# The start-up of a fused recurrent mixer and gated FFN: four token tiles normalised together, the first FFN step split into high and low parts, inverse roots by Newton steps, loads reordered

## The chip, the core and the metric

The kernel runs on one core of one Trainium2 chip. The metric is the device time of one execution in microseconds (us), the median of several runs. A core has five engines that run side by side, each with its own instruction queue worked off in order: the tensor engine (PE), VectorE (DVE), ScalarE (ACT), GpSimd (POOL) and SyncE (SP), which issues most of the DMA transfers. PE writes into PSUM, eight banks that the kernel hands out as small pools of tiles; the other engines work from PSUM and from the on-chip SBUF.

## The reference

A layer on x of 4 sequences x 256 tokens x 512 features. It is normalised, goes through a state-space mixer (128 heads, chunks, eight groups) and through a gated FFN whose weights are integers from -1 to 1 with a scale for each row; the product of both is added to x.

```python
def _layernorm(x, axis=-1, eps=1e-05):
    m = jnp.mean(x, axis=axis, keepdims=True)
    v = jnp.var(x, axis=axis, keepdims=True)
    return (x - m) / jnp.sqrt(v + eps)
...
gate_out = x_flat @ gate_w.T          # 1024 x 1792
up_out = x_flat @ up_w.T
hidden = jax.nn.silu(gate_out) * up_out
out_flat = hidden @ down_w.T
...
x = L0_attn_hidden_states
xn = _layernorm(x, axis=-1)
s = _L0_attn_ref(xn, ...)
g = _silu(_L0_ffn_ref(xn, ...))
x = x + s * g
```

The change touches the normalisation and the beginning of the FFN; the mixer is only moved in time with them.

## The kernel before

The 1024 tokens are 8 token tiles of 128 (`xts[0]` to `xts[7]`). The function `front` holds everything up to the FFN's end, about the first 300 us; the mixer's main loop over 64 tiles of channels follows it. Both are scheduled by hand: each engine works in the order in which the program issues to it.

**The entrance** (L519 to L550). SP loads x of tiles 0 to 3, the three weight blocks of FFN step 0 (`load_ffn(0)`: gate wg, up wu, down wd, each 256 KB of int32), two scale vectors, x of tiles 4 to 7, step 1's weights, the small constants, and `w` for the first mixer products. While x is on its way, PE runs matmuls on a tile of ones (`busy`, L270). The loop at L537 then normalises one tile after the other: statistics on DVE (`ln_stats`, L249 and L250), the root on ACT (`ln_std`, L253), the reciprocal on DVE (L542), the normalisation on DVE (`ln_norm`, L256), the transposition on PE (`ln_turn`, L264) into a PSUM tile. One turn later `split_tile` copies this into the high part xh on ACT (L283, rounded to the type that PE takes at full rate) and subtracts for the low part xl on DVE (L284). `keep` (L268) copies the transposed tile in full precision into `xnT` on ACT. The weight casts (`cast_ffn`, L230) run on POOL.

**The FFN steps** (L562 to L589). `steps` are 28: two halves of 512 tokens (tiles 0 to 3, then 4 to 7) by 14 blocks of 128 FFN features. A step multiplies wg with xh and xl into one PSUM bank (`project_exact`, L290: for each of four k a product with xh, then one with xl), takes Silu of it on ACT (L567), multiplies wu the same way, joins both on DVE (sg, L576), and splits sg into hh (ACT, L584) and hl (DVE, L588). The down product of a step (L298) comes two steps later, through `pending`. Each step issues the loads of step n + 2 at its head and the casts of step n + 1 in its middle. The pool `f2` of loaded weights holds two buffers for each of the three blocks.

**Other work between.** At three places of each step `next(pieces)` issues the next turn of a generator. Turns 0 and 1 (`first_pieces`, L385) are the statistics of tiles 4, 5 and 6, 7; turn 2 their common root on ACT, its reciprocal on DVE and the norm of tile 4; turn 3 the norm of tile 5; turns 4 and 5 the norms of tiles 6 and 7, and the transposition and keep of tiles 4 and 5; turns 6 and 7 the transposition and keep of tiles 6 and 7. These four transpositions share one PSUM bank (`ps_t`), so each waits until the keep before it has emptied it. From turn 6 on come the product with `wdt` and the steps of dt (`dt_pieces`), from turn 11 on the mixer's shared B and C blocks (`bc_pieces`).

Where turn 2 stands in a step, and what is queued around it:

```python
pu, wd = project_exact(ws[1], xh, xl), ws[2]
...
nc.vector.scalar_tensor_tensor(sg, pu, us[:, f:f + 1], sg, ALU.mult, ALU.mult)
if n + 1 < len(steps):
    ws = cast_ffn(n + 1)
next(pieces, None)
...
nc.scalar.copy(hh, sg)
...
next(pieces, None)
nc.vector.tensor_tensor(hl, sg, hh.bitcast(F32), ALU.subtract)
```

Of the kernel before, what the change touches and what calls it, by code (L numbers as in the profile page):

```python
# [43 lines left out]
F32 = mybir.dt.float32  # L44
F32R = mybir.dt.float32r
I32 = mybir.dt.int32
AF = mybir.ActivationFunctionType
ALU = mybir.AluOpType
PSUM = bass.MemoryType.PSUM

P = 128
# [4 lines left out]
NT = T // P  # L56
HID = 512
KT = HID // P
# [3 lines left out]
G = 8  # L62
# [3 lines left out]
CT = DIN // P  # L66
# [7 lines left out]
EPS = 1e-5  # L74
LEAD = 10
EARLY = 10
HALF = T // 2
# [5 lines left out]
def mixer_ffn(ctx: ExitStack, tc: tile.TileContext, x, in_w, conv_w, conv_b, dt_bias, a_log, d_col,  # L83
              norm_w, out_w, gate_t, up_t, down_t, gate_s, up_s, down_s, out):
    nc = tc.nc

    const = ctx.enter_context(tc.tile_pool(name="const", bufs=1))
    small = ctx.enter_context(tc.tile_pool(name="small", bufs=3))
    dram = ctx.enter_context(tc.tile_pool(name="dram", bufs=1, space=bass.MemoryType.DRAM))
    ps_proj = ctx.enter_context(tc.tile_pool(name="ps_proj", bufs=3, space=PSUM))  # L90
# [5 lines left out]
    eps = const.tile([P, 1], F32, name="eps")  # L96
# [5 lines left out]
    tiny = const.tile([P, 1], F32, name="tiny")  # L102
# [29 lines left out]
    def load_w(*tiles):  # L132
        w = wp.tile([P, 2, KT, P], F32, name="w")
        for n, i in enumerate(tiles):
            nc.sync.dma_start(w[:, n], in_w[i])
        return w
# [57 lines left out]
    def front(pre, one_of, fp, f2, hp, ep):  # L194
# [14 lines left out]
        bias = one_of.tile([P, 1], F32, name="bias")  # L209
# [4 lines left out]
        steps = [(h, f) for h in range(2) for f in range(FT)]  # L214
        loads = {}

        def load_ffn(n):
            f, ts = steps[n][1], []
            for tag, src in (("wg", gate_t[f]), ("wu", up_t[f]),
                             ("wd", down_t[f * P:(f + 1) * P, :])):  # L220
                wi = f2.tile([P, HID], I32, name=f"{tag}_i", tag=f"{tag}_i")
                nc.sync.dma_start(wi, src)
                ts.append((tag, wi))
            loads[n] = ts

        def cast_ffn(n):
            ws = []
            for tag, wi in loads.pop(n):
                w = fp.tile([P, HID], F32R, name=tag, tag=tag, bufs=4 if tag == "wd" else 2)
                nc.gpsimd.tensor_copy(w, wi)  # L230
                ws.append(w)
            return ws


        xts = []

        def load_x(ts):
            for t in ts:
                xt = pre.tile([P, HID], F32, name="xt")
                nc.sync.dma_start(xt, x[t * P:(t + 1) * P, :])  # L240
                xts.append(xt)

        mv = one_of.tile([P, NT, 2], F32, name="mv")
        rstd = one_of.tile([P, NT], F32, name="rstd")
        nc.scalar.activation(rstd[:, 0:1], eps, AF.Sqrt)

        def ln_stats(t):
            st = small.tile([P, 6], F32, name="st")
            nc.vector.bn_stats(st, xts[t])  # L249
            nc.vector.bn_aggr(mv[:, t, :], st)  # L250

        def ln_std(t, n=1):
            nc.scalar.activation(rstd[:, t:t + n], mv[:, t:t + n, 1], AF.Sqrt, bias=eps)  # L253

        def ln_norm(t):
            nc.vector.tensor_scalar(xts[t], xts[t], mv[:, t, 0:1], rstd[:, t:t + 1],  # L256
                                    ALU.subtract, ALU.mult)

        def ln_turn(t):

            p, tag = ((ps_o, "o"), (ps_y, "y"))[t // 2] if t < 4 else (ps_t, "t")
            tp = p.tile([P, KT, P], F32, name="tp", tag=tag)
            for k in range(KT):
                nc.tensor.transpose(tp[:, k, :], xts[t][:, k * P:(k + 1) * P], ident)  # L264
            return tp

        def keep(t, tp):
            nc.scalar.copy(xnT[:, :, t * P:(t + 1) * P], tp)  # L268

        def busy(n):  # L270

            for _ in range(n):
                nc.tensor.matmul(idle, ones, ones, start=True, stop=True)
# [4 lines left out]
        def split_x():  # L278
            return [hp.tile([P, KT, HALF], F32R, name=n) for n in ("xh", "xl")]

        def split_tile(xh, xl, t, v):
            to = slice(t % 4 * P, (t % 4 + 1) * P)
            nc.scalar.copy(xh[:, :, to], v)  # L283
            nc.vector.tensor_tensor(xl[:, :, to], v, xh[:, :, to].bitcast(F32), ALU.subtract)  # L284

        def project_exact(w, xh, xl):
            pp = ps_proj.tile([P, HALF], F32, name="pp", tag="proj")
            for k in range(KT):
                for part in (xh, xl):
                    nc.tensor.matmul(pp, w[:, k * P:(k + 1) * P], part[:, k, :],  # L290
                                     start=(k == 0 and part is xh),
                                     stop=(k == KT - 1 and part is xl))
            return pp
# [24 lines left out]
        held = {}  # L318
# [61 lines left out]
        def combine_x(n):  # L380

            a, b = ((x12, x11), (x22, xc[:, 0]), (x22, x12), (x21, xc[:, 1]))[n]
            nc.vector.tensor_sub(xc[:, n], a, b)

        def first_pieces():  # L385
            for t in range(4, NT):
                ln_stats(t)
                if t % 2:
                    yield
            ln_std(4, 4)  # L390
            nc.vector.reciprocal(rstd[:, 4:], rstd[:, 4:])
            ln_norm(4)
            yield
            ln_norm(5)
            yield
            for t in range(4, NT):
                if t + 2 < NT:
                    ln_norm(t + 2)
                keep(t, ln_turn(t))
                yield  # L400
            yield
            for n in range(4):
                combine_x(n)
                if n == 0:
                    held["a"] = combine_w(held.pop("w"))
                yield
# [113 lines left out]
        load_ffn(0)  # L520
        nc.sync.dma_start(gs, gate_s)
        nc.sync.dma_start(us, up_s)
        load_x(range(4, NT))
        load_ffn(1)
        nc.sync.dma_start(wdt, in_w[PROJ // P - 1])
        nc.sync.dma_start(bias, dt_bias)
        nc.sync.dma_start(a_neg, a_log)
        for to, src in ((cw, conv_w), (cb, conv_b), (dcol, d_col), (nw, norm_w)):
            nc.sync.dma_start(to, src)
        nc.sync.dma_start(ds_bc, down_s.partition_broadcast(P))  # L530
        held["w"] = load_w(2 * CT + G, 2 * CT)

        idle = ps_t.tile([P, P], F32, name="idle", tag="t")
        xh, xl = split_x()
        busy(8)
        ws, tps = cast_ffn(0), []
        for t in range(5):  # L537
            if t < 4:
                ln_stats(t)
                ln_std(t)  # L540
            if t:
                nc.vector.reciprocal(rstd[:, t - 1:t], rstd[:, t - 1:t])  # L542
                ln_norm(t - 1)
                tps.append(ln_turn(t - 1))
                busy(4)
            if t > 1:
                split_tile(xh, xl, t - 2, tps[t - 2])
        split_tile(xh, xl, 3, tps[3])
        for t in range(4):
            keep(t, tps[t])  # L550
        pending = []

        def down_next():
# [6 lines left out]

        pfs = None
        for n, (h, f) in enumerate(steps):  # L562
            if n + 2 < len(steps):
                load_ffn(n + 2)
            pg = project_exact(ws[0], xh, xl)
            sg = fp.tile([P, HALF], F32, name="sg")
            nc.scalar.activation(sg, pg, AF.Silu, scale=gs[:, f:f + 1])  # L567
            if f == 2 and h:
                ffn_out(h - 1, pfs, (2, 3))
            next(pieces, None)  # L570
            pu, wd = project_exact(ws[1], xh, xl), ws[2]
            if f == FT - 1 and h == 0:
                xh, xl = split_x()
                for t in range(4, NT):
                    split_tile(xh, xl, t, xnT[:, :, t * P:(t + 1) * P])
# [4 lines that stand above are left out]
            if len(pending) == 2:  # L580
                down_next()
            hh = fp.tile([P, HALF], F32R, name="hh")
            hl = fp.tile([P, HALF], F32R, name="hl")
            nc.scalar.copy(hh, sg)  # L584
            if f == 1 and h:
                ffn_out(h - 1, pfs, (0, 1))
            next(pieces, None)
            nc.vector.tensor_tensor(hl, sg, hh.bitcast(F32), ALU.subtract)  # L588
            pending.append((f, hh, hl, wd))  # L589
        w = load_w(1, CT + 1)  # L590
# [6 lines left out]

    with (tc.manual_schedule(), tc.tile_pool(name="pre", bufs=NT) as pre,
          tc.tile_pool(name="one_of", bufs=1) as one_of, tc.tile_pool(name="fp", bufs=3) as fp,
          tc.tile_pool(name="f2", bufs=2) as f2, tc.tile_pool(name="hp", bufs=1) as hp,  # L600
          tc.tile_pool(name="ep", bufs=3) as ep):
        a, w = front(pre, one_of, fp, f2, hp, ep)

# [211 lines left out]
    with tc.manual_schedule():  # L815
# [4 lines left out]
        for i in range(CT):  # L820
# [32 lines left out]
            if 0 < i < CT - 1:  # L853
                w = load_w(i + 1, CT + i + 1)
# [204 lines left out]
        for n in range(2):  # L1059
            two, to = slice(2 * n, 2 * n + 2), slice(n * HALF, (n + 1) * HALF)  # L1060
# [3 lines left out]
        for n in range(2):  # L1064
            to = slice(n * HALF, (n + 1) * HALF)
# [97 lines left out]
```

## Time and profile before

| what | value |
|---|---|
| runs | 1721.35, 1721.91, 1725.25 us; median 1721.91 |
| profiled execution, span from its first to its last instruction | 1719.7 us |
| first product of FFN step 0 (xh) | 12.72 us |
| first product of FFN step 2 | 23.10 us |
| last down product of the FFN | 300.6 us |
| granted clock of PE | 1.00 |

The span is one execution taken by the profiler, in us from its first instruction; the runs are whole device times and so a little longer. The profile's own time outside the span is not listed, so its distance to the median, 2.2 us, is taken as what lies around it. In the profile's lines PE is the matmuls, PEld the weight loads that overlap them, DVE VectorE, ACT ScalarE, POOL GpSimd, SPq the queue of SP. "out<-in" are the program's tile names, and L264 is line 264 of the kernel. A matmul of 128x512 in the fast type follows the one before it after 0.2265 us, though a single one is listed with 0.39 us, as they are pipelined; a 128x512 product in full float32 is listed as two.

### The profile page before, as it was taken

The numbers are of one execution on the slowest core, as the hardware profiler recorded it, in microseconds if no ns is written. First come the engines' busy times: TensorE is split into PE (matmuls) and PEld (weight loads), VectorE is DVE, ScalarE is ACT, GpSimd is POOL, SyncE is SP. The second block draws the span as 40 slices with busy tenths as digits, with TensorE's granted clock in tenths as the row PEclk, the third lists the DMA queues.
The fourth block names the chain that finished last, engine by engine and source line by source line (L and its number), as shares of the span: only waits on it lengthen the run. The fifth ranks groups of instructions, "written<-read, shape, count | busy, mean of one in ns | idle before, by whom it ended". The sixth has DMA issues, their size and how long they took to land.

```text
span 1719.7 us, 22509 instructions
## 1 busy us (share of the span) xinstructions
PE 1707.3 (99%) x8458; PEld 1098.6 (64%) x8458; DVE 1448.2 (84%) x1742; ACT 1071.0 (62%) x1434; POOL 216.9 (13%) x238
## 2 busy tenths in 40 slices
PE   8999999999999999999999999999999999999999
PEld 6666667555566666666666666666666666666687
DVE  5768787788898898889888988898889988898876
ACT  4544333688766667666766666667666666666640
POOL 3223323000000000100011100110111011101110
PEclk9999999999999999999999999999999999999999
DMA  7257565676756675767676767776766677767775
GB/s 230 89 168 247 208 232 201 209 218 211 238 189 206 195 216 174 202 200 211 181 207 201 215 192 211 205 217 191 212 202 197 194 204 197 207 179 210 208 220 178
DMA packets 161931, 347.27 MB, mean 202 GB/s; under 512 B 15136, under 2 KB 52896, under 8 KB 161824
## 3 DMA queue, kind: packets, MB, share of 16 engines
q1 hardware_dynamic: 139136, 292.89, 49.4%
q0 software_dynamic: 22688, 52.96, 17.3%
q8 instruction: 67, 1.10, 0.3%
q14 instruction: 40, 0.33, 0.1%
HBM read 236.48 MB, written 81.00 MB: 185 GB/s over the span
## 4 chain that ended last, share of the span: by engine, by line
PE 93%; DVE 3%; DMA 1%; ACT 1%; issue 1%; SPq 0%; ACTq 0%; DVEq 0%
PE px L175 28%; PE po L775 22%; PE pq L175 14%; PE py L694 10%; PE pz L175 7%; PE pp L290 5%; PE tp L650 3%; PE pf L298 2%; PE pg L470 1%; DVE cT L183 1%; DMA m<-rows 1%; DMA gated<-yg 0%; PE pd L323 0%; DVE m L644 0%; DMA wd_i<-in_down_t 0%
## 5 line engine op out<-in xcount | busy, mean ns | idle before, releaser
L175 PE MATMUL px<-xc,w 128*128 128x512 f32 x576 | 271.3, 593 | 0.0
L183 DVE SCALAR_TENSOR_TENSOR xT<-xpad,cw,xT 128x1024 f32<-128x1024 f32 x192 | 246.2, 1282 | 10.7 <-ACT xT L179 6.4
L191 DVE TENSOR_TENSOR_SCAN m<-m,after 128x1024 f32<-128x1024 f32 x108 | 246.5, 2282 | 1.0 <-DMA m<-rows 1.0
L775 PE MATMUL po<-wo,ya 128*128 128x256 f32 x768 | 176.5, 379 | 0.0
L644 DVE TENSOR_TENSOR m<-m,gm 128x1024 f32<-128x1024 f32 x128 | 150.7, 1219 | 14.9 <-ACT m L636 14.9
L694 PE MATMUL py<-m,v 128*64 128x128 f32 x2048 | 160.7, 276 | 0.4 <-DVE v L667 0.4
L913 POOL DMA_DIRECT2D sqacc<-sq x54 | 46.1, 853 | 876.0 <-ACT sq L909 835.2
L775 PEld LDWEIGHTS po<-wo,ya 128*128 128x128 f32 x768 | 141.5, 190 | 17.0 <-issue 0.2
L175 PE MATMUL pz<-xnT,w 128*128 128x512 f32 x288 | 145.8, 592 | 0.0
L175 PEld LDWEIGHTS px<-xc,w 128*128 128x128 f32 x576 | 99.3, 190 | 72.2 <-issue 68.9
L175 PE MATMUL px<-xnT,w 128*128 128x512 f32 x288 | 141.8, 615 | 0.0
L175 PE MATMUL pq<-xnT,s 128*128 128x512 f32 x288 | 136.3, 595 | 1.4 <-DVE xpad L945 1.4
L175 PE MATMUL px<-xc,s 128*128 128x512 f32 x288 | 135.7, 594 | 1.8 <-ACT cpad L433 1.6
L175 PE MATMUL pq<-xc,s 128*128 128x512 f32 x288 | 135.3, 592 | 0.0
L636 ACT ACTIVATE m<-m 128x1024 f32<-128x1024 f32 x128 | 134.3, 1058 | 0.6
L650 PEld LDWEIGHTS tp<-ident,xT 128*128 128x128 f32 x512 | 67.8, 141 | 99.5 <-issue 87.9
L694 PEld LDWEIGHTS py<-m,v 128*64 128x64 f32 x2048 | 117.6, 137 | 21.0 <-issue 19.1
L775 PE MATMUL po<-tw,sy 128*128 128x256 f32 x512 | 115.9, 379 | 0.0
L775 PEld LDWEIGHTS po<-tw,sy 128*128 128x128 f32 x512 | 97.2, 190 | 13.2
L883 ACT COPY gT<-px 128x512 f32<-128x512 f32 x64 | 37.5, 586 | 106.2 <-PE px L175 106.2
L694 PE MATMUL py<-mo,v 128*64 128x128 f32 x1024 | 99.7, 273 | 0.0
L175 PEld LDWEIGHTS pq<-xc,s 128*128 128x128 f32 x288 | 54.7, 190 | 68.9 <-issue 61.9
(187 smaller groups left out, 3105.6 us busy)
## 6 DMA issues: line engine op xcount, KB each, us to landing
m<-rows SPq DMA_DIRECT2D x108, 512.0 KB, 6.6
w<-in_in_w SPq DMA_DIRECT2D x144, 256.0 KB, 6.9
mo<-rows SPq DMA_DIRECT2D x128, 256.0 KB, 7.4
gated<-yg SPq DMA_DIRECT2D x64, 512.0 KB, 8.5
ya<-gated SPq DMA_DIRECT2D x30, 1024.0 KB, 7.1
sqacc<-sq POOLq DMA_DIRECT2D x54, 512.0 KB, 6.3
wo<-in_out_w SPq DMA_DIRECT2D x64, 256.0 KB, 6.9
acc<-sa POOLq DMA_DIRECT2D x23, 512.0 KB, 5.8
```

What stands on the lines that cost most here:

```text
L175: nc.tensor.matmul(pp, a[:, k, :], b[:, k, :], start=start and k == 0, stop=k == KT // 2 - 1, skip_group_check=not start)
L183: nc.vector.scalar_tensor_tensor(xT, xpad[:, :, k:k + L], cw[:, i, k:k + 1], xT, ALU.mult, ALU.add)
L191: nc.vector.tensor_tensor_scan(m, m, after, 0.0, ALU.add, ALU.mult)
L290: nc.tensor.matmul(pp, w[:, k * P:(k + 1) * P], part[:, k, :], start=(k == 0 and part is xh), stop=(k == KT - 1 and part is xl))
L298: nc.tensor.matmul(pf, part[:, i * P:(i + 1) * P], wd, start=(f == 0 and part is hh), stop=(f == FT - 1 and part is hl))
L636: nc.scalar.activation(m, m, AF.Exp)
L644: nc.vector.tensor_mul(m, m, gm[:, 0:T])
L650: nc.tensor.transpose(tp[:, b, :], xT[:, b, c * P:(c + 1) * P], ident)
L694: nc.tensor.matmul(py[d, q * P:(q + 1) * P], v[:, b, h, :], m, start=False, stop=True, skip_group_check=True)
L775: nc.tensor.matmul(po, a[:, k, :], b[:, k, :], start=start and k == 0, stop=k == HG - 1, skip_group_check=not start)
L883: nc.scalar.copy(gT[:, HALF:], px)
L913: nc.gpsimd.dma_start(sqacc, sq, accum_op=ALU.add)
```

## The change

1. **Entrance.** The loop now runs only statistics, roots, inverses and norms of the four tiles; the norm of tile 2 goes to GpSimd. The casts of step 0 stand behind it. Then, in a loop of its own, tiles are transposed, with filler matmuls between (none after the last), and split. An activation on a 128x1 tile asks for the Silu table right after the last split, and only tiles 0 and 1 are kept before the first product; tiles 2 and 3 are kept after the Silu of step 0.
2. **Step 0.** Its two banks are filled by all eight products with xh, then all eight with xl.
3. **Tiles 4 to 7.** Root and reciprocal are replaced on VectorE by a first guess from the bits (three operations) and three Newton rounds of three operations, on 128x4.
4. **Loads.** Step 1's weights go ahead of x 4 to 7; step 2's weights and `w` go right behind, ahead of `wdt` and the constants. Each step issues the loads of step n + 3; `f2` has three buffers.

```diff
+        def ln_inverse(t):
+            nc.vector.reciprocal(rstd[:, t:t + 1], rstd[:, t:t + 1])
+        def ln_norm(t, engine=nc.vector):
+            engine.tensor_scalar(xts[t], xts[t], mv[:, t, 0:1], rstd[:, t:t + 1],
+                                 ALU.subtract, ALU.mult)
+        def rstd_begin(to, v):
+            nc.vector.tensor_scalar(v, v, EPS, None, ALU.add)
+            bits = to.bitcast(I32)
+            nc.vector.tensor_scalar(bits, v.bitcast(I32), 1, None, ALU.logical_shift_right)
+            nc.vector.tensor_scalar(bits, bits, -1, 0x5f375a86, ALU.mult, ALU.add)
+        def rstd_refine(to, v):
+            y2 = small.tile([P, NT // 2], F32, name="y2")
+            nc.vector.scalar_tensor_tensor(y2, to, -0.5, to, ALU.mult, ALU.mult)
+            nc.vector.tensor_mul(y2, y2, v)
+            nc.vector.scalar_tensor_tensor(to, y2, 1.5, to, ALU.add, ALU.mult)
...
+        def project_part(pp, w, part, first):
+            for k in range(KT):
+                nc.tensor.matmul(pp, w[:, k * P:(k + 1) * P], part[:, k, :],
+                                 start=first and k == 0, stop=not first and k == KT - 1)
...
-            ln_std(4, 4)
-            nc.vector.reciprocal(rstd[:, 4:], rstd[:, 4:])
+            to, v = rstd[:, 4:], mv[:, 4:, 1]
+            rstd_begin(to, v)
+            for _ in range(3):
+                rstd_refine(to, v)
             ln_norm(4)
...
+        load_ffn(1)
         load_x(range(4, NT))
-        load_ffn(1)
+        load_ffn(2)
+        held["w"] = load_w(2 * CT + G, 2 * CT)
         nc.sync.dma_start(wdt, in_w[PROJ // P - 1])
...
-        held["w"] = load_w(2 * CT + G, 2 * CT)
...
+        for t in range(4):
+            ln_stats(t)
+            ln_std(t)
+            if t:
+                ln_inverse(t - 1)
+                ln_norm(t - 1, nc.gpsimd if t == 3 else nc.vector)
+        ln_inverse(3)
+        ln_norm(3)
         ws, tps = cast_ffn(0), []
-        for t in range(5):
-            if t < 4:
-                ln_stats(t)
-                ln_std(t)
-            if t:
-                nc.vector.reciprocal(rstd[:, t - 1:t], rstd[:, t - 1:t])
-                ln_norm(t - 1)
-                tps.append(ln_turn(t - 1))
+        for t in range(4):
+            tps.append(ln_turn(t))
+            if t < 3:
                 busy(4)
-            if t > 1:
-                split_tile(xh, xl, t - 2, tps[t - 2])
-        split_tile(xh, xl, 3, tps[3])
-        for t in range(4):
+            split_tile(xh, xl, t, tps[t])
+        nc.scalar.activation(tiny, eps, AF.Silu)
+        for t in range(2):
             keep(t, tps[t])
+        first = [proj_bank() for _ in range(2)]
+        for part in (xh, xl):
+            for pp, w in zip(first, ws):
+                project_part(pp, w, part, part is xh)
...
-            if n + 2 < len(steps):
-                load_ffn(n + 2)
-            pg = project_exact(ws[0], xh, xl)
+            if n + 3 < len(steps):
+                load_ffn(n + 3)
+            pg = project_exact(ws[0], xh, xl) if n else first[0]
...
+            if n == 0:
+                for t in range(2, 4):
+                    keep(t, tps[t])
...
-            pu, wd = project_exact(ws[1], xh, xl), ws[2]
+            pu, wd = project_exact(ws[1], xh, xl) if n else first[1], ws[2]
...
-          tc.tile_pool(name="f2", bufs=2) as f2, tc.tile_pool(name="hp", bufs=1) as hp,
+          tc.tile_pool(name="f2", bufs=3) as f2, tc.tile_pool(name="hp", bufs=1) as hp,
```

More of the change, by code (lines that the diff above doesn't have):

```diff
@@ L250, in ln_stats, with ln_std @@
             nc.vector.bn_aggr(mv[:, t, :], st)
[L252 to L257, printed above, removed]
+        def ln_std(t):
+            nc.scalar.activation(rstd[:, t:t + 1], mv[:, t, 1:2], AF.Sqrt, bias=eps)
+        def ln_inverse(t):
[13 more added lines that the diff above has]
+            nc.vector.scalar_tensor_tensor(to, y2, 1.5, to, ALU.add, ALU.mult)
         def ln_turn(t):
@@ L284, in split_tile, with proj_bank @@
             nc.vector.tensor_tensor(xl[:, :, to], v, xh[:, :, to].bitcast(F32), ALU.subtract)
+        def proj_bank():
+            return ps_proj.tile([P, HALF], F32, name="pp", tag="proj")
+        def project_part(pp, w, part, first):
+            for k in range(KT):
+                nc.tensor.matmul(pp, w[:, k * P:(k + 1) * P], part[:, k, :],
+                                 start=first and k == 0, stop=not first and k == KT - 1)
         def project_exact(w, xh, xl):
-            pp = ps_proj.tile([P, HALF], F32, name="pp", tag="proj")
+            pp = proj_bank()
             for k in range(KT):
```

## The prediction

> **What bounds the kernel.** I read the busy table first, then busy time by stretch, then the waits of the tensor engine (PE), then the chain that ended last around the edited lines, and at last the instructions there in order of time.
>
> ```profile
> span 1719.7 us, 22509 instructions
> PE 1707.3 (99%) x8458; PEld 1098.6 (64%) x8458; DVE 1448.2 (84%) x1742; ACT 1071.0 (62%) x1434; POOL 216.9 (13%) x238
> ```
>
> PE is busy for all but 12.4 us. The stretches say where these are (after the stretch: its length, PE busy, PEld, DVE, ACT, POOL, granted clock, DMA share, GB/s).
>
> ```profile
> 0.00:13.40 13.40, 10.18 (x66) 9.15 (x66) 9.37 (x22) 5.60 (x12) 5.45 (x19) 1.00 0.85 289
> 13.40:20.50 7.10, 7.10 (x31) 5.70 (x31) 4.01 (x11) 5.63 (x9) 0.84 (x2) 1.00 0.91 265
> 20.50:23.10 2.60, 1.20 (x9) 0.83 (x9) 2.60 (x5) 2.23 (x4) 2.24 (x3) 1.00 0.88 316
> 23.10:130.00 106.90, 106.79 (x413) 71.60 (x412) 68.26 (x80) 52.05 (x67) 29.05 (x33) 1.00 0.42 138
> ```
>
> Outside the start-up only 20.5 to 23.1 is poor. From 23.1 on PE runs without a gap to speak of: what the edit gains or loses before the third FFN step (first matmul 23.10) moves everything behind it by as much, and nothing later gives it back. So I need one number, that of this matmul. The waits of PE in the first 300 us agree:
>
> ```profile
> PE tp L264 <- DVE xt L256: 2.2, 3, 0.9
> PE px L175 <- ACT cpad L433: 1.6, 2, 1.4
> ...
> PE tp L264 <- ACT xnT L268: 1.0, 1, 1.0
> PE pp L290 <- DVE xl L284: 0.2, 1, 0.2
> ```
>
> All but the second are at edited lines, and no wait for a weight cast is among them. The chain in order of time (start, us, what) shows what held the second gap:
>
> ```profile
> 13.36 3.70 PE pp L290 x15
> ...
> 17.15 0.76 DVE sg L576
> ...
> 17.93 0.62 ACT hh L584
> ...
> 18.57 1.28 ACT L253
> ...
> 19.87 0.30 ACT rstd L253
> ...
> 20.18 1.28 ACT L567
> ...
> 21.48 0.69 ACT sg L567
> 22.16 0.48 ACT xnT L268
> ...
> 22.69 0.66 PE tp L264 x4
> ```
>
> Two table loads (L253 for the root, L567 for the Silu) stand on ScalarE (ACT) between the first step's product and the transposition of token tile 5.
>
> **Part 1, the entrance.** Today VectorE (DVE) does xl of tiles 0 and 1 between the statistics. From the timeline: norm of tile 1 ends at 6.81 + 0.55 = 7.36. With xl moved back, statistics of tile 3 start there; aggregation follows 0.72 later (8.17 to 8.89 today), the inverse of tile 2 0.09 after that, 0.13 long: 8.30. The norm of tile 2 is now on GpSimd (POOL), which starts 0.07 after its releaser (memset end 2.00, select 2.07): 8.37. The trace has no such operation on POOL. The nearest are the 128x512 casts, 0.61 us undisturbed (7.43) and 1.16 us at 20.86, beside DVE's norms; as DVE's norm of tile 3 falls at 8.79 to 9.34, right beside it, I take 0.92, between the two. It ends at 9.29 (8.98 to 9.53), and the transposition starts 0.06 later, 9.35 (9.04 to 9.59). Behind it the distances of today hold: 1.51 to the last transposition (9.79 to 11.30, the four filler matmuls in it), 0.69 to its xh copy, 0.70 to the first product (11.99 to 12.69). So the first product starts at 12.25 (11.94 to 12.49). Today it starts at 12.69, but the second then waits for xl until 13.36; at 0.2265 us a matmul (13.93 to 14.16 and on) that is worth a start at 13.13. In the new order eight products on the high parts come first, to 14.06, and the last xl is there at 12.86, so that wait is gone. **Gain 0.88 (0.64 to 1.19).**
>
> On the GpSimd engine the Trainium skill (GPSIMD Engine Reference, 3.1 Elementwise) has a rule that speaks against this part: elementwise work is to stay on VectorE, and an add of 2048 fp32 took 1.96 times as long on GPSIMD. By it the norm would be an estimated 1.96 x 0.55 = 1.08 us, and the gain 0.72 instead of 0.88; no row of this trace shows it.
>
> Costed at nothing, with the cover: POOL's casts of step 0 now stand behind that norm, wg done by 9.29 + 0.61 = 9.9 and wu by 10.6, against needs at 12.25 and 13.16; uncovered they would cost their lateness. The filler matmuls after the last transposition go; nothing waited on them. The early Silu table load (1.28) and a 0.2 us activation run from 12.15 to 13.65, two keeps of 0.59 to 14.83, and the first Silu is due at 15.24. The other two keeps come behind it and are read at 25.48.
>
> **Part 2, tiles 4 to 7.** DVE works in order: statistics 4 and 5, the product sg of step 0, statistics 6 and 7, then the inverse roots, norm 4, hl. Let sg start at S. Today S = 17.15, the aggregation of tile 7 starts at S + 2.18 (19.33) and is 0.18 long, the reciprocal runs at 20.20 because the root on ACT waits for its table until 19.85, norm 4 ends at 20.96, tile 4 is transposed at 21.07 = S + 3.92. PE ran dry at 20.51.
> New: root, reciprocal and two table loads go (ACT: 1.28 + 0.30 + 1.28). In come 12 operations on 128x4, each on the one before: 3 to begin and 3 rounds of 3. No such operation is in the trace. Start to start, a 128x1 reciprocal and its dependent norm are 0.17 apart (5.14 to 5.31), the 128x4 one 0.21 (20.20 to 20.41). Below, two small ones that don't depend are 0.10 apart (5.04 to 5.14); above, a 128x4 activation took 0.297. I take d = 0.18, nearest the two dependent rows. Then norm 4 starts at S + 2.18 + 0.18 + 0.03 + 12 x 0.18 = S + 4.55, and tile 4 is transposed 0.55 + 0.11 later, at S + 5.21: 1.29 later against S than today.
> Given back: the keep of tile 4 no longer stands behind a Silu that waits for its table. Today tile 5 follows tile 4 by 1.62 (21.07 to 22.69); undisturbed it is 0.65 to the copy plus 0.63 to the next transposition, 1.28. **Part 2 costs 1.29 - 0.34 = 0.95.** S itself is 12.25 + 15 x 0.2265 + 0.50 = 16.15 (today 16.65 to 17.15), so the third step starts at 16.15 + 5.21 + 1.28 + 0.41 = 23.05, against 23.10. Queued behind the chain on DVE are hl of step 0 (0.69, read by PE only at 31.12), norm 5 (0.55) and sg of step 1 (0.75): 21.25 + 1.99 = 23.24. For that wait hh on ACT (0.62) and, behind it, the keep of tile 5 (0.58): 24.5. It frees the bank for tile 6, which PE reaches after eight products at 23.05 + 1.8 = 24.85. So 0.35 is left, and as PE moves with the chain it stays so for other d; without this cover each us late would cost one.
>
> The Trainium skill (ScalarE: Activation LUTs, What ACT_TABLE_LOAD costs) gives a switch of table 1283 ns plus a drain of some 1380 ns. The trace has the 1.28, but the root follows its load at 19.87, 0.02 after it, so the drain isn't there. By the page the edit would take an estimated 5.3 us off ACT, by the rows 2.86 with the root; either way the time moves only as far as DVE's chain lets it.
>
> **Part 3, the loads.** SP issues x 4 to 7 behind step 1's three loads: three of 0.43 from 5.13, then x at some 0.4 to 0.65 each, x4 from 6.4, x7 from 8.4. The median landing of x is 4.1, the longest of any load here 5.7: x4 by 10.5 to 12.1, x7 by 12.5 to 14.1. Wanted by DVE at 12.87 and at 17.6. Step 2's loads and w go ahead of wdt (read at 25.48) and of the small constants (cw first read at 64). From then on each FFN load is a step earlier, on a third buffer; load n + 3 waits for cast n, as load n + 2 did, so SP is held no longer. POOL waited 113 us in all for wg loads in the first 300, but the weight loads of PE waited for casts 0.7 in all (0.5 for wg, 0.2 for wd). I put this part at nothing; if x4 came later than 12.87 + 1.7 (what DVE has to spare before S), each us would cost one.
>
> **The sum.** 12 d - 1.21 - gain of part 1 = 2.16 - 1.21 - 0.88 = +0.07 us on a span of 1719.7. Around the span lie 2.2 us up to the median of 1721.91 (single runs to 1725.25). Forecast 1722.0: no change. Ends: 12 x 0.10 - 1.21 - 1.19 = -1.2 and 12 x 0.297 - 1.21 - 0.64 = +1.7, so 1720.7 to 1723.6. What a measurement of this kernel can tell is some 0.2%, 3.4 us.
>
> **Rivals.** *Faster*: the small operations run 0.10 apart, POOL takes 0.61 (-1.2), and the earlier loads and freed ACT also remove the one other gap, 1.4 us where px waits for cpad at 135. That gives -2.6, 1719.3. For it: the gap exists and ACT waits for DVE there; against: DVE is what lags, and no load is in that wait. *Slower*: the 12 operations on DVE in front of norm 4. Even from d = 0.174 they eat all of part 1; at 0.297 and a slow POOL it is +1.7, 1723.6; to be seen beyond 0.2% d would have to be 0.455, more than any small row here. For it: strictly dependent, and PE is dry by 19.50 with nothing else in its queue; against: both dependent rows lie near 0.2. *The loads don't do what they say*: x4 arrives late behind 0.75 MB more. At the 332 GB/s moved between 11 and 13.4 these are 2.3 us, with the longest landing 6.4 + 5.7 + 2.3 = 14.4, just inside the 14.57. It decides from there; 1.5 us later, at 15.9 or so, it turns +0.07 into +1.4, 1723.4. Against: today the last of the same bytes (wd of step 1) landed at 13.92, and x4 is the fourth last of them.
>
> **How the numbers follow.** Forecast 0.64, faster rival 0.16, slower chain 0.13, late loads 0.07. No case reaches 3.4 us by its own price; with the scatter of single runs (3.9 us between three) I leave 0.09 for faster and 0.08 for slower beyond 0.2%, 0.83 for within. Range 1719.3 to 1724.3: the faster rival's price to the slower ones' with 0.7 for scatter.
>
> **What would show it.** First product on xh near 12.25 and no wait at the first xl; no table load between the first and third steps; tile 4 transposed near 21.4, with PE idle some 1.9 before it, put down to DVE's norm; the third step's first product near 23.05. The prediction is wrong if the small operations are far from 0.18, if POOL's norm takes over 1.2, if the granted clock falls in that longer gap (1.00 throughout today), or if a stage after 130 us moves.

## The result and the profile after

| | median of runs | lowest to highest | runs |
|---|---|---|---|
| before, the three runs above and five timed along with it | 1725.02 us | 1721.35 to 1726.27 | 8 |
| after | 1727.91 us | 1726.99 to 1731.76 | 8 |

The ratio after to before is **1.0029, 95% interval 1.0019 to 1.0038**: some 5 us slower (0.0029 x 1722), between 3.3 and 6.5. The two medians of the table lie only 2.9 apart, and in experiment 8, against 33 runs of the kernel before, 5.9 at a ratio of 1.0025; so the loss is clear, and its size is known to a few us. The forecast was 1722.0 and no change; the time lies 3.6 us above the top of the range. The profiled execution has a span of 1727.5 us inside a run of 1729.25: some 1.7 us lie around it where the prediction took 2.2.

The page's busy table of the changed kernel (engine, busy us, share of the span, instructions):

```profile
span 1727.5 us, 22499 instructions
PE 1711.0 (99%) x8450; PEld 1101.7 (64%) x8450; DVE 1449.1 (84%) x1752; ACT 1068.7 (62%) x1432; POOL 215.5 (12%) x239
```

PE's busy time grew by 3.7 us while it has eight instructions fewer. More busy time for less work is a sign of a slower clock. The rest, 7.8 - 3.7 = 4.1 us, is new idle time. Two of the stretches of the changed kernel, with the same bounds and columns as for the kernel before:

```profile
...
20.50:23.10 2.60, 0.48 (x3) 0.05 (x1) 2.33 (x9) 0.00 (x0) 1.82 (x3) 1.00 0.99 372
23.10:130.00 106.90, 105.29 (x395) 70.27 (x395) 66.26 (x81) 49.70 (x64) 25.47 (x29) 0.97 0.41 135
```

In the first of them PE has 0.48 us left of 1.20, and ACT, which had been busy 2.23, does nothing: the table loads are gone, and nothing came of it. The second shows 0.97 where 1.00 was granted before. Stretches of 2 us say where the clock fell (the third value from the end):

```profile
...
22.00:24.00 2.00, 0.11 (x1) 0.14 (x2) 1.89 (x5) 0.00 (x0) 0.95 (x2) 0.97 0.99 371
24.00:26.00 2.00, 1.32 (x6) 0.92 (x7) 2.00 (x5) 0.99 (x2) 0.00 (x0) 0.50 1.05 402
26.00:28.00 2.00, 2.00 (x8) 1.71 (x7) 0.97 (x2) 0.70 (x2) 0.00 (x0) 0.50 1.06 394
...
30.00:32.00 2.00, 2.00 (x8) 1.35 (x7) 0.00 (x0) 1.28 (x2) 0.62 (x1) 0.82 0.04 10
```

Half clock follows the gap of PE, 21.0 to 23.9, at once, and lasts for some 6.8 us. The waits of PE in the first 300 us (total us, times, longest):

```profile
PE tp L279 <- DVE xt L259: 3.9, 2, 2.9
PE px L175 <- ACT cpad L458: 3.1, 3, 1.4
...
PE pp L306 <- ACT xh L298: 0.8, 1, 0.8
```

The wait for xl (0.2 before) is gone. In its place the first product waits 0.8 for ACT's last copy to xh, as no filler matmuls follow the last transposition any more. The wait for DVE's norm grew from 2.2 to 3.9, and that of px for cpad from 1.6 to 3.1.

**Where the loss arises**, by the start of the same PE work in the two profiled executions: last product of the second FFN step +0.31 (20.28 to 20.59); transposition of tile 4 +2.79 (21.10, its first matmul, to 23.89); first product of the third step +3.32 (23.10 to 26.42); product with `wdt` +5.29 (25.48 to 30.77); then +5.3 up to 168; +6.05 behind the gap at 170; +6.65 behind the one at 230; +6.8 from 261 on; +7.2 from 296 on; +7.8 at the end.

Three rows of the timeline of the changed kernel show the entrance (start, us, engine, line, operation, tiles, shape, idle time before):

```profile
8.34 2.08 POOL L259 TENSOR_SCALAR xt<-xt,mv,rstd 128x512 f32<-128x512 f32 x1 [4.62 <-DVE rstd L256]
8.74 0.63 DVE L259 TENSOR_SCALAR xt<-xt,mv,rstd 128x512 f32<-128x512 f32 x1
...
13.44 1.17 PE L306 MATMUL pp<-xh,wg 128*128 128x512 f32 x4 [0.77 <-ACT xh L298]
```

A norm of the same shape takes VectorE 0.63 and GpSimd 2.08. The next rows, of DVE, POOL and PE, show the Newton chain and the gap:

```profile
19.85 0.17 DVE L263 TENSOR_SCALAR mv<-mv 128x4 f32<-128x4 f32 x1
...
21.05 0.16 DVE L270 SCALAR_TENSOR_TENSOR y<-rstd 128x4 f32<-128x4 f32 x1
21.07 0.63 POOL L230 CAST wg<-wg_i 128x512 fp32r<-128x512 int32 x1 [2.41 <-PE pp L313]
21.25 0.46 DVE L271 TENSOR_TENSOR y<-y,mv 128x4 f32<-128x4 f32 x1
...
22.34 0.62 POOL L230 CAST wd<-wd_i 128x512 fp32r<-128x512 int32 x1
22.43 0.53 DVE L271 TENSOR_TENSOR y<-y,mv 128x4 f32<-128x4 f32 x1
...
23.20 0.55 DVE L259 TENSOR_SCALAR xt<-xt,mv,rstd 128x512 f32<-128x512 f32 x1
23.89 1.08 PE L279 MATMUL tp<-ident,xt 128*128 128x128 f32 x4 [2.91 <-DVE xt L259]
```

Up to 21.05 the small operations run 0.20 apart. Each that starts inside a weight cast of GpSimd takes 0.46 to 0.53 and ends as the cast does: 21.25 + 0.46 = 21.71, against 21.07 + 0.63 = 21.70. Three of them make the chain 3.35 long instead of 2.4.

That VectorE is slower beside a cast could be read in the timeline of the kernel before: the norm of tile 5, which takes 0.55 by itself, ran there beside casts (the first from 20.86 to 22.02).

```profile
21.48 0.83 DVE L256 TENSOR_SCALAR xt<-xt,mv,rstd 128x512 f32<-128x512 f32 x1
```

### The profile page after: what moved, and what is told of

It reads as the page before. It is cut to its first block, busy times and chain, and to the rows that moved or that the text cites. A ratio compares the mean times of both kernels' runs of the same rounds, so it can differ in the third digit from the quotient of the medians.

```text
span 1727.5 us, 22499 instructions
## 1 busy us (share of the span) xinstructions
PE 1711.0 (99%) x8450; PEld 1101.7 (64%) x8450; DVE 1449.1 (84%) x1752; ACT 1068.7 (62%) x1432; POOL 215.5 (12%) x239
## 4 chain that ended last, share of the span: by engine, by line
PE 91%; DVE 5%; DMA 3%; issue 1%; ACT 1%; SPq 0%; ACTq 0%; DVEq 0%
PE px L175 27%; PE po L810 22%; PE pq L175 14%; PE py L729 10%; PE pz L175 7%; PE pp L313 4%; PE tp L685 3%; PE pf L321 2%; DVE cT L183 1%; PE pg L495 1%; DMA m<-rows 1%; DMA gated<-yg 0%; DVE em L191 0%; DMA ya<-gated 0%; PE pd L346 0%
## 5 line engine op out<-in xcount | busy, mean ns | idle before, releaser
L729 PEld LDWEIGHTS py<-m,v 128*64 128x64 f32 x2048 | 117.6, 137 | 21.2 <-issue 19.1
L175 PEld LDWEIGHTS px<-xc,s 128*128 128x128 f32 x288 | 54.3, 190 | 70.5 <-issue 63.6
```

The source lines that it names most:

```text
L175: nc.tensor.matmul(pp, a[:, k, :], b[:, k, :], start=start and k == 0, stop=k == KT // 2 - 1, skip_group_check=not start)
L729: nc.tensor.matmul(py[d, q * P:(q + 1) * P], v[:, b, h, :], m, start=False, stop=True, skip_group_check=True)
```

## The experiments

They ran in three series, each with its own runs of the kernel before (medians 1722.42, 1722.05 and 1722.81). Diffs are against the changed kernel, in the last two against the kernel before. PE's gap is that ahead of tile 4's transposition, in the profiled execution.

**1. Norm of tile 2 on VectorE.**

```diff
-                ln_norm(t - 1, nc.gpsimd if t == 3 else nc.vector)
+                ln_norm(t - 1)
```

> The changed kernel with one part undone: the norm of token tile 2 runs on VectorE again. In the changed kernel it took 2.08 us on GpSimd (8.34 to 10.42) against 0.55 on VectorE. Theory (the entrance lost 1.5 us to the GpSimd norm, and a gap of PE later, with a clock drop behind it, lost the rest): the norm ends near 8.9, the first product starts at 11.9 to 12.2 instead of 13.44, the step after that is as long as before, so 1.2 to 1.5 us less than the changed kernel (ratio to the kernel before 1.0020 to 1.0022), with the PE gap ahead of tile 4 still 2.5 us or more. Rival (the GpSimd norm is hidden behind the filler matmuls, which set the transposition at 10.74 anyway): first product not before 13.1, ratio 1.0027 or more.

Measured: 1727.18, ratio 1.0027 (1.0016 to 1.0038). The first product starts at 11.39 instead of 13.44. A part of that is x, which arrived 0.23 earlier in this execution; counted from the norm of tile 1, the first product comes 4.80 later (11.39 - 6.59) instead of 6.62 (13.44 - 6.82; 6.42 in 8). So the entrance is 1.6 to 1.8 us shorter without GpSimd's norm. The Newton chain, now ahead of the casts, took 2.38 (17.79 to 20.17); PE's gap was 1.96, less than expected, and the clock still fell to 0.50 behind it, for 3.4 us. The place is shown; the time cannot decide, as the interval holds the changed kernel's ratio too, and in the profiled execution PE also waited 3.1 us near 472, behind a late load of `m`, with half clock for another 3.4 us.

**2. Root of tiles 4 to 7 back on ACT.**

```diff
-            rstd_begin(to, v)
-            for _ in range(3):
-                rstd_refine(to, v)
+            nc.scalar.activation(rstd[:, 4:], mv[:, 4:, 1], AF.Sqrt, bias=eps)
+            nc.vector.reciprocal(rstd[:, 4:], rstd[:, 4:])
```

> The changed kernel with one part undone: the inverse roots of tiles 4 to 7 are a root on ScalarE and a reciprocal again, table loads included. Theory (12 dependent small operations on VectorE, 3.35 us instead of 1.1, leave PE idle for 2.9 us, and the granted clock then falls to 0.50 for 6.8 us): tile 4 is transposed some 3.9 to 4.1 us after sg of step 0 starts instead of 6.44, the gap is 0.5 to 0.7 us, the clock stays at 1.00, and the time falls by 4 to 5 us against the changed kernel, to a ratio of 1.0000 to 1.0006. Rival 1 (the clock drop has another cause, such as the entrance): only 2.5 to 3.3 us less and the half clock is still there near 24 us. Rival 2 (the loads or the later gaps at 170 and 230 us cost the time): less than 2 us.

Measured: 1723.66, ratio 1.0006 (0.9997 to 1.0014), granted clock 1.000 in 10 of 11 runs. Tile 4 is transposed at 20.90, 3.96 behind the start of sg (3.95 before the change, 21.10 - 17.15). Most of the loss goes with the chain. The gaps ahead of px at 165 and 225 remain, 0.85 and 0.79.

**3. Loads as before.**

```diff
-        load_ffn(1)
         load_x(range(4, NT))
-        load_ffn(2)
-        held["w"] = load_w(2 * CT + G, 2 * CT)
+        load_ffn(1)
...
-            if n + 3 < len(steps):
-                load_ffn(n + 3)
+            if n + 2 < len(steps):
+                load_ffn(n + 2)
...
-          tc.tile_pool(name="f2", bufs=3) as f2, tc.tile_pool(name="hp", bufs=1) as hp,
+          tc.tile_pool(name="f2", bufs=2) as f2, tc.tile_pool(name="hp", bufs=1) as hp,
```

(`held["w"]` goes back behind the constants.)

> The changed kernel with one part undone: order of the loads, two buffers and loads two steps ahead as in the kernel before. Theory (the loads cost nothing themselves, but by landing early they let GpSimd cast the weights of step 3 during the Newton operations, of which three took 0.46 to 0.53 instead of 0.16): the Newton chain shrinks from 3.35 to some 2.5 us, the gap ahead of tile 4 from 2.9 to 2.1, 0.8 us less; if 2.1 us is short of what drops the clock, another 2 us less (ratio 1.0013 to 1.0025). Rival 1 (the loads are not involved): within 0.5 us of the changed kernel, ratio 1.0027 to 1.0032, operations of 0.46 still there. Rival 2 (the gaps at 170 and 230 us come from the new loads): these gaps of 0.9 and 0.8 us vanish too, 1.3 us or more less.

Measured: 1727.44, ratio 1.0031 (1.0020 to 1.0043). The opposite of what was expected at the start: the weights of the third step now land later, so its casts and those of the fourth, all six, fall onto the chain (19.94 to 23.8), and it takes 4.52 (20.11 to 24.63), with a gap of 4.08 and 6.8 us of half clock. But the gaps at 171 and 231 are gone (0.27 at most). So the new load order helps the chain and makes the later gaps.

**4. and 5. Filler matmuls in the gap**, into a spare tile, 24 and then 9 of them, to keep the clock up.

```diff
+            if t == 4:
+                more = ps_t.tile([P, P], F32, name="idle", tag="t")
+                for _ in range(9):
+                    nc.tensor.matmul(more, ones, ones, start=True, stop=True)
```

> The changed kernel plus 24 filler matmuls on the tile of ones ahead of the transposition of tile 4 (2.6 us at full clock), nothing else. Theory (the clock drop after the 2.9 us gap costs 2 to 2.7 us by itself, apart from the gap): granted clock 1.00 from 20 to 35 us, third step's first product at 25.6 to 25.9 instead of 26.42, and the time 2 to 3 us below the changed kernel, ratio 1.0012 to 1.0019. Rival (the clock makes no difference to the end, because VectorE is what lags): same as the changed kernel, 1.0027 to 1.0032.

> The changed kernel plus 9 filler matmuls ahead of the transposition of tile 4. With 24 they took 5.3 us (two records of 0.11 each) and held PE until 27.14, 3.6 us after the norm of tile 4 was done; 9 are 2.0 us, so they fit into the gap. Theory (the clock drop costs 2 to 3.4 us in each run by itself, apart from the gap): clock 1.00 in nearly all runs, tile 4 transposed as soon as its norm is done, the time 2 to 3.4 us under that of the changed kernel in this same series. Rival (without the overlong filler the clock still makes no difference): within 1 us of it.

Measured: with 24, 1729.02, ratio 1.0037 (1.0025 to 1.0049). They are listed as 48 matmuls and last 5.5 us (from 21.56), so they held tile 4 to 27.14 while its norm ended at 23.52; the clock stayed at 1.00, but as a price this run is inconclusive. With 9: 1725.41, ratio 1.0015 (1.0006 to 1.0024), clock 0.999 to 1.000 in all runs. They last from 20.68 to 22.85, tile 4 follows at 22.98. Against the unchanged kernel of the same series (8) that is 2.5 us less by medians. The intervals overlap, so this is a likely price of the clock, not a sharp one; and in the profiled execution the casts came late, too: the first started at 21.94, behind the start of the last small operation (21.89).

**6. 1 and 2 together.**

> The changed kernel with two parts undone: the norm of tile 2 on VectorE and the root of tiles 4 to 7 on ScalarE. The new entrance, the split first step and the loads stay. Theory: first product at 11.4 to 11.9 (worth 13.13 in the kernel before), tile 4 transposed 3.9 to 4.0 us after sg starts as in the kernel before, third step near 21.4 to 21.9 instead of 23.10, clock 1.00: ratio 0.9990 to 0.9995. Rival (the entrance gains nothing that lasts): ratio 1.0000 to 1.0006, as with the ScalarE root alone.

Measured: 1722.83, ratio 1.0006 (0.9997 to 1.0015). First product 11.65, tile 4 at 19.61, third step near 21.6, or 1.5 ahead of the kernel before. By the positions of the same PE work the gaps at 164 and 224 take 0.72 and 0.60 of it back, and 0.10 near 254 and 0.44 near 290 follow: from there on this execution is 0.36 behind. The early gain is real and is lost in the main loop.

**7. As 1, and all statistics of tiles 4 to 7 in the first turn**, so that the chain starts right behind sg.

```diff
                 ln_stats(t)
-                if t % 2:
-                    yield
+            yield
+            yield
```

> The changed kernel with the norm of tile 2 on VectorE and the statistics of tiles 6 and 7 moved ahead of sg of step 0, into the 1.8 us in which VectorE sits idle there; the Newton steps stay. Theory (Newton costs because 1.6 us of statistics and 2.4 us of small operations stand between sg and the norm of tile 4): the norm ends 3.7 us after sg starts instead of 5.3, the gap ahead of tile 4 is 0.2 to 0.6 us, no table load remains there, the clock stays at 1.00, third step at 20.6 to 21.0: ratio 0.9984 to 0.9990. Rival (x of tiles 6 and 7 is not there in time): sg slips by 0.5 us or more and the ratio is above 0.9992.

Measured: 1722.61, ratio 1.0001 (0.9992 to 1.0010). Newton from 16.02, tile 4 at 19.49 with a gap of only 0.61 although the Newton steps stay, third step near 21.2: 1.9 ahead of before. The lead is again given back, by 0.72, 0.60, 0.12 and 0.44 near 164, 224, 254 and 290, where the execution is level with the one before (+0.03). Near 472 it then waits 2.7 us behind a load of `m`, followed by 3.4 us of half clock, and is 2.5 behind from there on. The time expected was missed.

**8. The changed kernel again**, as it is.

> The changed kernel itself, for comparison within this series. Theory: clock 0.998 to 0.999 in every run, ratio 1.0025 to 1.0035, the small operations 0.20 apart where no weight cast on GpSimd runs beside them. Rival (the half clock of its profile was one execution's chance): clock 1.000 in half the runs or more.

Measured: 1727.90, ratio 1.0025 (1.0016 to 1.0034), so the result repeats. The runs list clocks from 0.997 to 1.000, where 0.998 or 0.999 had been expected in every run. The two at 1.000 took 1724.49 and 1726.28; the six at 0.997 and 0.998 have a median of 1728.6. The profiled execution was the fastest of them (span 1722.8), and its timeline shows the start-up without the drop:

```profile
22.03 0.55 DVE L259 TENSOR_SCALAR xt<-xt,mv,rstd 128x512 f32<-128x512 f32 x1
...
22.73 0.63 PE L279 MATMUL tp<-ident,xt 128*128 128x128 f32 x4 [1.95 <-DVE xt L259]
```

GpSimd's norm takes 2.08 again (from 8.36). The casts came only at 22.80, behind the chain, which took 2.38 (19.65 to 22.03); the gap was 1.95 and the clock stayed at 1.00. So how much the change costs in one execution hangs on when the fourth step's weights land: their first cast stood at 21.07 in the execution shown above, and here it waited for its load until 22.80.

**9. 7 with the loads of 3**: the fast norm, early statistics, Newton, and the old load order.

> The kernel with the statistics first and the norm of tile 2 on VectorE, and in addition the loads as in the kernel before (order, two buffers, two steps ahead). With the new loads its third step began 1.9 us earlier than in the kernel before, but its time was the same: new gaps of 0.9 and 0.8 us stood at 165 and 225 us, where px waits for cpad. Theory (the loads a step ahead let GpSimd cast beside VectorE's convolution steps, which makes VectorE late there, 1.5 us in all): both gaps fall to 0.3 us or less, third step at 20.9 to 21.4, ratio 0.9985 to 0.9993. Rival (these gaps come with any earlier start, as VectorE then has less of a lead): gaps of 0.8 us stay, ratio 0.9998 to 1.0004.

Measured: 1721.13, ratio 0.9993 (0.9982 to 1.0005), profiled span 1718.3. Rows of its waits of PE:

```profile
PE px L175 <- ACT cpad L458: 1.6, 2, 1.4
PE tp L279 <- DVE xt L259: 1.3, 2, 1.1
```

px waits 1.6 as before the change, tile transpositions 1.3 for DVE instead of 2.2, and the gap ahead of tile 4 is 0.23, with the Newton steps in place. It has the lowest median of all versions, 1.7 us under the kernel before, but the interval reaches past 1: whether it is faster is not settled.

**10. 6 with the loads of 3**: the new entrance, with VectorE's norm, and nothing else.

> The kernel before with the new entrance and split first step alone, the norm of tile 2 on VectorE: root of tiles 4 to 7 on ScalarE, loads as before. Theory: third step at 21.4 to 21.8, no gap over 0.4 us at 165 and 225, clock as in the kernel before, ratio 0.9988 to 0.9995. Rival (as for the kernel with the statistics first): gaps stay, ratio 1.0002 to 1.0008.

Measured: 1722.51, ratio 0.9998 (0.9987 to 1.0008). First product 11.82, third step near 21.8, no gap at 165 or 225. In the profile the gap theory holds: up to 440 this execution is 1.3 to 1.8 ahead of the one before. Near 472 it waits 3.0 us behind a load of `m` (1.2 in the kernel before), and the lead is gone. That wait is between 0.3 and 3.1 in the executions profiled here. The time is level with the kernel before.

**11. The kernel before with Newton only** (the four lines of 2 put in the other way).

> The kernel before with one part of the change: root and reciprocal of tiles 4 to 7 replaced by the Newton steps. Theory: tile 4 transposed 5.3 us after sg starts without GpSimd casts beside the small operations, 6.5 or more with them; as the loads of step 2 land near 20.9 there, two or more casts fall into the Newton steps and the gap of PE is 2 to 4 us, the clock drops in most runs: ratio 1.0018 to 1.0032, clock 0.998 to 0.999. Rival (Newton is harmless by itself, its cost came from the GpSimd norm or the loads): ratio under 1.0008, clock 1.000.

Measured: 1727.52, ratio 1.0023 (1.0014 to 1.0031), clock 0.997 to 0.998 in all 12 runs. Rows of its timeline (DVE's Newton and POOL's casts, mixed by time):

```profile
20.13 0.61 POOL L230 CAST wg<-wg_i 128x512 fp32r<-128x512 int32 x1 [5.83 <-DMA wg_i<-in_gate_t]
20.24 0.51 DVE L267 SCALAR_TENSOR_TENSOR y<-rstd 128x4 f32<-128x4 f32 x1
...
20.79 0.64 POOL L230 CAST wu<-wu_i 128x512 fp32r<-128x512 int32 x1
20.98 0.46 DVE L269 SCALAR_TENSOR_TENSOR rstd<-y,rstd 128x4 f32<-128x4 f32 x1
...
24.20 0.55 DVE L256 TENSOR_SCALAR xt<-xt,mv,rstd 128x512 f32<-128x512 f32 x1
```

Six casts from 20.13 to 23.95 stand beside the chain, and an operation in it takes up to 0.59. The chain takes 4.57 (19.63 to 24.20), PE's gap is 4.13 and the clock stays at 0.50 for 6.8 us. Newton alone, with nothing of the entrance, gives +4.0 of the some 5 us. With experiment 2, where the loss goes when the steps go, that makes the Newton chain, where it stands, with the gap and the clock behind it, the main cause. It is worse placed here than in the change, as all six casts fall onto it, three there; so the 4.0 is not simply its share of the 5.

**12. The kernel before with the new load order only** (the diff of 3 the other way).

> The kernel before with one part of the change: the order of the loads, three buffers, loads three steps ahead. Theory: start-up as before (third step at 23.0 to 23.2), gaps of 0.8 to 0.9 us at 167 and 226 us in front of px, 1.3 to 1.7 us in all: ratio 1.0007 to 1.0010. Rival (the loads cost nothing): ratio 0.9997 to 1.0003, no new gap.

Measured: 1723.92, ratio 1.0005 (0.9996 to 1.0013). The start-up is as before, and the gaps appear: 0.85 at 165 and 0.78 at 225. A row of its waits:

```profile
PE px L175 <- ACT cpad L433: 3.0, 3, 1.4
```

3.0 instead of 1.6, so the load order alone makes these gaps. By the positions of the same PE work this execution is level with the one before up to 165, 0.69 behind from there, 1.27 behind from 226, 1.4 from 256 and 1.83 from 291 on. The changed kernel loses the same 1.9 between 148 and 300 (+5.34 to +7.20). (The last step, 0.44, also came in 3, with the old order, and so may have another cause.) In the time such an amount lies inside the interval and is not resolved.

How it makes them is seen when the same part of the main loop is laid side by side. The kernel before, rows of DVE and POOL in its timeline:

```profile
156.41 0.61 POOL L230 CAST wg<-wg_i 128x512 fp32r<-128x512 int32 x1 [12.18 <-DMA wg_i<-in_gate_t]
...
159.75 2.88 DVE L183 SCALAR_TENSOR_TENSOR cT<-cpad,cw,cT 128x1024 f32<-128x1024 f32 x2
162.55 0.69 DVE L588 TENSOR_TENSOR hl<-sg,hh 128x512 fp32r<-128x512 f32 x1
```

And the changed kernel, some 5.4 us later throughout, with the product that waits:

```profile
165.17 3.11 DVE L183 SCALAR_TENSOR_TENSOR cT<-cpad,cw,cT 128x1024 f32<-128x1024 f32 x2
165.60 1.60 POOL L230 CAST wg<-wg_i 128x512 fp32r<-128x512 int32 x1
167.16 1.60 POOL L230 CAST wu<-wu_i 128x512 fp32r<-128x512 int32 x1
168.20 1.09 DVE L623 TENSOR_TENSOR hl<-sg,hh 128x512 fp32r<-128x512 f32 x1
...
171.24 1.13 PE L175 MATMUL px<-xc,s 128*128 128x512 f32 x2 [0.90 <-ACT cpad L458]
```

Before, the cast of wg waited for its load and ran at 156.41, ahead of the convolution. With weights there a step earlier, casts fall beside VectorE's convolution: they take 1.60 instead of 0.61, the first two steps of cT 3.11 instead of 2.88, hl 1.09 instead of 0.69. VectorE ends 0.63 later (0.23 + 0.40), ACT's copy to cpad waits for it, and PE for that.

## Why the prediction was wrong, step by step

The step that failed most is the price of the Newton chain in Part 2: 12 d = 2.16, at most 3.56, with nothing for casts of GpSimd beside the chain and nothing for a slower clock behind the longer gap. The runs showed a chain of 3.35 to 4.57 beside casts, and some 2 to 2.8 us more from the clock. Two smaller terms failed as well: GpSimd's norm, and the loads that were put at nothing.

- **Part 1, GpSimd's norm (0.92, from 0.61 to 1.16): failed.** It measured 2.08 in all six profiled executions that had it. The first product came at 13.44 instead of 12.25, and a gain of 0.88 turned into a loss of 0.31. The bounds were casts with one input and no pointer operands; the norm takes a mean and a root per partition, and no row showed that on GpSimd. Whether this makes the 2.08, or VectorE's norm of tile 3 that ran beside it each time, was not tested. The Trainium skill (GPSIMD Engine Reference, 3.1 Elementwise) was right in its advice to keep elementwise work on VectorE, but its 1.96, measured on an add, is too low for this norm: 2.08 / 0.55 = 3.8.
- **Part 1, the order of products: right.** There is no wait at the first xl. With VectorE's norm the entrance gains what was hoped, and more: first product at 11.4 to 11.8 in experiments 1, 6, 7, 9 and 10, where 12.25 had been predicted with GpSimd's.
- **Part 2, d = 0.18: mis-sized, and its upper bound failed.** Undisturbed, the 12 operations take 2.38, 0.198 each, near the estimate. But 12 x 0.297 = 3.56 was given as the most, and beside casts it is 3.35, 4.52 and 4.57 (after, 3, 11). The step never asked what GpSimd does in these 2 us. It had read that a cast beside VectorE took 1.16 instead of 0.61, but not that VectorE is slower beside a cast, as the 0.83 at 21.48 showed. As the prediction said, "to be seen beyond 0.2% d would have to be 0.455, more than any small row here"; in experiment 11 the mean was 4.57 / 12 = 0.38, and the clock did the rest.
- **Part 2, S + 5.21 for tile 4: wrong by 1.23**, it was S + 6.44, with PE idle for 2.91 instead of 1.9. About 1.0 of it are the casts (3.35 - 2.38) and 0.2 the size of d; without casts it was S + 5.48 (experiments 1 and 8). S itself came at 17.45 instead of 16.15, 1.19 of that at the first product, from GpSimd's norm. The 1.28 from tile 4 to tile 5 was near (1.31 in experiments 1 and 5).
- **The granted clock: named as what would make it wrong, and given no price.** Half speed for 6.8 us sets products 0.427 apart instead of 0.2265 (27.42, 27.84, 28.27, 28.70 in the timeline after). From the third step to the product with `wdt` it took 4.35 instead of 2.38, which is +1.97; from tile 4 to the third step 2.53, where 1.28 + 0.41 was predicted. So 2 to 2.8 us of this execution are the clock's, in line with the 2.5 of experiment 5. "1.00 throughout today" was one execution: in the third series 5 of the 35 runs of the kernel before list 0.998 (median 1726.9), 16 list 1.000 (median 1721.95). The Trainium skill (TensorE: Matmul & The Clock Gate, What's actually happening) has the clock halve after an idle window of about 3.4 us that runs free of the program. Here it fell after gaps shorter than that, of 1.96 (1) and 2.91, and not after gaps of 1.95 (8) and 2.99 (10, near 472); so a gap of 3.4 is not needed, and up to 3 us its length alone does not decide. The half clock lasted 3.4 or 6.8 us, one or two times the window of the page.
- **"So 0.35 is left ... it stays so for other d": right for the waits**, and what happened ahead of the third step was carried unchanged from 30.77 to 168 (+5.29 to +5.35). "Nothing later gives it back" did not hold for a lead: 6, 7 and 10 lost theirs at the gaps of the load order or at the wait near 472.
- **Part 3 "at nothing": half right.** x 4 to 7 came in time. But the cover named was the wait for the casts, and the casts themselves were not asked about; moving them a step earlier cost the two gaps, 0.9 + 0.8 by the waits, +1.3 in position by 237 and +1.9 by 300.
- **The rivals.** The slower one had the right place and mechanism, the operations on DVE in front of norm 4, and the wrong point from which it decides, as it counted neither contention nor clock. The faster one was wrong on its second half: the early loads lengthened the wait of px for cpad. The late loads did not happen.

The prediction's two ways of adding up differ by 0.12 (the third step 0.05 ahead, the sum 0.07 behind), which changes nothing. The measured sum, for the profiled executions: +3.32 at the third step (+1.30 at S, nearly all GpSimd's norm, chain +1.23, the clock in the transpositions +0.84, all against the prediction's own steps), +1.97 for the clock up to `wdt`, +1.9 between 148 and 300, as with the load order alone in 12. The last 0.6 comes near 456, 472 and 1640, at waits that differ from one execution to the next. Not tried: to keep GpSimd's casts off the chain, or to use fewer Newton rounds.

## What to carry to other kernels

Work that is cheap by itself has to be costed beside what the neighbouring engine does in the same microseconds: a chain of twelve small operations went from 2.4 us to 4.5 beside casts. Where an edit lengthens a gap of TensorE to about 2 us or more, as here, put a price on the slower clock that can follow it, here 2 to 3 us. A load that lands earlier also moves the work that it releases: look at what that work then runs beside.

## What the runs showed of the hardware

- A tensor_scalar of 128x512 float32 with two per-partition operands took 2.08 us on GpSimd, beside VectorE's work, and 0.55 on VectorE undisturbed (0.63 beside GpSimd's norm, 0.83 beside a cast).
- A 128x4 operation of VectorE went from 0.16 to 0.46 to 0.60 if it started beside a 128x512 cast of GpSimd, and ended with the cast. Casts went from 0.61 to 1.60 beside VectorE's convolution. The Trainium skill (SBUF – State Buffer, Who interferes with whom) has these two engines share a pair of ports that one holds at a time; the paired end times fit that.
- The clock fell to 0.50 for 3.4 or for 6.8 us at single gaps of PE of 1.96 to 4.13 us, and not in every execution of the same kernel.
- The filler matmul of 128x128 float32 is listed as two of about 0.12 us each (2.17 us for 9, 5.5 us for 24).
